# A four-layer graph network on one core: node sums in float32r, the edge softmax moved out of the main path, and another form of the attention block

## Chip, cores and metric

The kernel runs on one core of a Trainium2 chip. The metric is the time of one execution in microseconds (us) of device time. One profiled execution gives the trace that all readings below come from.

## The reference

There are 32 graphs of 512 nodes with 128 features, and one adjacency matrix of 512 x 512 zeros and ones with a full diagonal. Four layers follow each other; each ends in `x = layernorm(x + layer(x))`.

```python
# layer 0 (and layer 1 alike: other weights, no b, elu for the last leaky_relu)
h = x @ W;  e_src = h @ a_src;  e_dst = h @ a_dst
logits = leaky_relu(e_src[:, :, None] + e_dst[:, None, :], 0.2)
alpha = softmax(where(adj > 0, logits, -1e9), axis=-1)
out = leaky_relu(alpha @ h + b, 0.3)
# layer 2: an edge softmax A (512 x 512) from the edge weights e, the same for all graphs
A = softmax(where(adj > 0, e[rank of the edge], -9e15), axis=1)
out = (A * eye) @ (x @ W[0]) + (A * (1 - eye)) @ (x @ W[1]) + bias
# layer 3
y = (adj @ x + x) @ weight + bias
out = y / max(norm(y), 1e-12)
```

In the given inputs all edge weights `e` are one, so that a row of A holds the same value, one over the number of neighbours, at each edge.

## The kernel before

A graph is four chunks of 128 nodes (`NCH = 4`, 128 partitions each) of 128 features. Each graph is a Python generator, `graph(b)`, which records the instructions of one stage between two `yield`s. The loop at the end of the main path advances all running graphs by one stage per round, oldest first, and starts a new graph every second round (`STEP = 2`). So in the middle of the run, some eleven graphs are in flight, and one period of the kernel is two rounds, in which each layer's work is done for one graph. The framework's scheduler then fixes the order of each engine's queue; every engine takes its own instructions in that order, and waits on semaphores where they need another engine's result.

The stages, with their lines:

- `attention(k, b, xi)`, layers 0 and 1. Four transposes of x on TensorE (L288), a copy from PSUM on ScalarE (`xt`, L290). The product with the weights, which carry three more columns for the attention terms (`ph`, L295), and one exponential of these columns (`exps`, L297). ScalarE scales the 128 columns of h per node (L303), and GpSimd copies a column of exponentials beside them (L300). Transposes of a broadcast column give the row term (`pr`, L309). VectorE makes the 512 x 512 attention block in four steps `al` of 128x512 (L312), each the maximum of the row term and a per-node term, times the mask `mt`. Sixteen products (L318) give the weighted sums and, as column 129, their denominators. VectorE divides (L321, then L325 or L328) and applies the activation (L326, or L331 on ScalarE and L333), and GpSimd adds x (L334).
- `norm_stats` and `normalise` end each layer: statistics on VectorE (L262, L263), the power of -1/2 and the bias on GpSimd (four small instructions, L266 to L269), and four scaled copies on ScalarE (L274).
- `layer2`: products with the diagonal part `dg` of the edge softmax (L358), node sums with its other part `at` in `aggregate` (L348, `py`), copies on ScalarE (L360, L350), products with both weights (L366, L367), the bias on VectorE (L369), and x on GpSimd (L370).
- `layer3`: node sums with `a3t`, the transposed adjacency plus the identity (L348), the product (L387), the bias (L389), squares with their sum on ScalarE (L394), the norm on GpSimd (L396, L397), and the scaled sum with x on VectorE (L400).

A node sum is four products of 128x128 by 128x512 in float32. The edge softmax is worked out once, in round 5, by `edge_softmax()`, for any edge weights: ranks of the edges by running sums (L212), one-hot products (L224, L237), and a softmax of each row; `a3t` is transposed in round 9.

If an exponential leaves a wide range, or a diagonal entry is missing, the flag that `outside()` computes sends the program at its end (L614) into `general_path`, which does all graphs again in another way. With the given inputs that path does not run.

Of the kernel before, what the change touches and what calls it, by code (L numbers as in the profile page):

```python
# [23 lines left out]
F32 = mybir.dt.float32  # L25
I32 = mybir.dt.int32
AF = mybir.ActivationFunctionType
# [3 lines left out]
P = 128  # L31
# [5 lines left out]
def kernel(  # L37
# [87 lines left out]
    def attention_weights(k, w, a_src, a_dst):  # L125
# [11 lines left out]
        nc.vector.tensor_scalar(we[:, F + 2 : FE], q[:, 1:2], -0.8, None, op0=ALU.mult)  # L137
# [5 lines left out]

    exps = const.tile([P, B * 2, NCH, 3], F32, name="exps")

    def transposed(dst, src, name, add_ident=False):

        for jc in range(NCH):
            p = ps1(f"{name}_{jc}")
            for ic in range(NCH):  # L150
                nc.tensor.transpose(p[:, ic * P : (ic + 1) * P], src[:, ic, jc * P : (jc + 1) * P], ident)
            if jc % 2:
                nc.vector.tensor_copy(dst[:, jc, :], p)
            else:
                nc.scalar.copy(dst[:, jc, :], p)
            if add_ident:
                d = dst[:, jc, jc * P : (jc + 1) * P]
                nc.vector.tensor_add(d, d, ident)
# [6 lines left out]
    loops = const.tile([P, NCH, P], F32, name="loops")  # L165
    for c in range(NCH):
        nc.gpsimd.tensor_mul(loops[:, c, :], em[:, c, c * P : (c + 1) * P], ident)

    def edge_softmax():
# [63 lines left out]
        dg = const.tile([P, NCH, P], F32, name="dg")  # L233
# [19 lines left out]
        at = const.tile([P, NCH, N], F32, name="at")  # L253
        transposed(at, a, "pa")
        return at, dg

    def norm_stats(r, name, small=small):

        st = small.tile([P, NCH, 6], F32, tag="st", name=f"st{name}")
        mv = small.tile([P, NCH, 2], F32, tag="mv", name=f"mv{name}")  # L260
        for c in range(NCH):
            nc.vector.bn_stats(st[:, c, :], r[:, c, :])  # L262
            nc.vector.bn_aggr(mv[:, c, :], st[:, c, :])  # L263
        rstd = small.tile([P, NCH], F32, tag="rstd", name=f"rstd{name}", bufs=8)
        nmr = small.tile([P, NCH], F32, tag="nmr", name=f"nmr{name}", bufs=8)
        nc.gpsimd.tensor_scalar(rstd, mv[:, :, 1], EPS, None, op0=ALU.add)  # L266
        nc.gpsimd.tensor_tensor(rstd, rstd, mhalf, op=ALU.pow)  # L267
        nc.gpsimd.tensor_mul(nmr, mv[:, :, 0], rstd)  # L268
        nc.gpsimd.tensor_scalar(nmr, nmr, -1.0, None, op0=ALU.mult)  # L269
        return rstd, nmr  # L270

    def normalise(xo, r, rstd, nmr):
        for c in range(NCH):
            nc.scalar.activation(xo[:, c, :], r[:, c, :], AF.Identity, bias=nmr[:, c : c + 1], scale=rstd[:, c : c + 1])  # L274

    def new_x(k, b):
        return work.tile([P, NCH, F], F32, tag=f"x{k}", name=f"x{k}_{b}", bufs=3)

    def new_o(n):
        return work.tile([P, NCH, F], F32, tag="o", name=f"o{n}", bufs=5)  # L280


    def attention(k, b, xi):
        n = f"{k}_{b}"
        we = ATT[k]
        p = ps1(f"pt{n}")
        for c in range(NCH):
            nc.tensor.transpose(p[:, c * P : (c + 1) * P], xi[:, c, :], ident)  # L288
        xt = work.tile([P, N], F32, tag="xt", name=f"xt{n}", bufs=3)
        nc.scalar.copy(xt, p)  # L290
        yield

        ph = ps2(f"ph{n}")
        for c in range(NCH):
            nc.tensor.matmul(ph[:, c, :FE], xt[:, c * P : (c + 1) * P], we, start=True, stop=True)  # L295
        ex = exps[:, 2 * b + k]
        nc.scalar.activation(ex, ph[:, :, F:FE], AF.Exp)  # L297

        h = work.tile([P, NCH, F + 1], F32, tag="h", name=f"h{n}", bufs=3)
        nc.gpsimd.tensor_copy(h[:, :, F], ex[:, :, 1])  # L300
        for c in range(NCH):
            pc = ex[:, c, 1:2]
            nc.scalar.activation(h[:, c, :F], ph[:, c, :F], AF.Identity, bias=pc if k else 0.0, scale=pc)  # L303
        yield


        pr = ps1(f"pr{n}")
        for c in range(NCH):
            nc.tensor.transpose(pr[:, c * P : (c + 1) * P], ex[:, c, 0:1].to_broadcast([P, P]), ident)  # L309
        al = work.tile([P, NCH, N], F32, tag="al", name=f"al{n}", bufs=3)  # L310
        for j in range(NCH):
            nc.vector.scalar_tensor_tensor(al[:, j, :], pr, ex[:, j, 2:3], mt[:, j, :], op0=ALU.max, op1=ALU.mult)  # L312
        yield

        po = ps2(f"po{n}")
        for c in range(NCH):
            for j in range(NCH):
                nc.tensor.matmul(po[:, c, : F + 1], al[:, j, c * P : (c + 1) * P], h[:, j, :],  # L318
                                 start=(j == 0), stop=(j == NCH - 1))
        rs = small.tile([P, NCH], F32, tag="rs", name=f"rs{n}")  # L320
        nc.vector.reciprocal(rs, po[:, :, F])  # L321
        o = new_o(n)
        if k == 0:
# [83 lines left out]
    def graph(b):  # L407
        xi = yield from attention(0, b, X0.pop(b))
        xi = yield from attention(1, b, xi)
        if b == B - 1:  # L410
            outside()
# [235 lines left out]
```

## Time and profile before

| what | value |
|---|---|
| median of 3 runs | 797.29 us (795.61 to 797.82) |
| the profiled execution | 797.82 us; its span, first to last instruction, 796.1 us |
| granted TensorE clock, mean | 0.975 |
| TensorE products, busy | 731.8 us, 92% of the span |
| VectorE | 535.5 us, 67% |
| ScalarE | 451.7 us, 57% |
| GpSimd | 416.2 us, 52% |
| mean DMA rate | 24 GB/s |

In the lines of the profile, PE is TensorE, PEld its weight loads, DVE VectorE, ACT ScalarE, POOL GpSimd and SP the engine that issues most transfers; L12 is line 12 of the kernel file. A timeline line has the start and the length in us, then engine, line, operation, names, sizes and how many instructions were merged into it; in square brackets stands how long the engine had been idle before it, and who released it. A busy share is an average over stages with different limits: what a stage is worth is read from that stage.

### The profile page before, as it was taken

Reading aid. Unit: us, or ns where it says so; the run is one execution under the profiler, and the core shown is the slowest. Engines: PE = TensorE matmul, PEld = TensorE weight load, DVE = VectorE, ACT = ScalarE, POOL = GpSimd, SP = SyncE. Lnnn points to the kernel's source line nnn. Section 1 sums busy time; section 2 is a strip of 40 time slices with the busy share of each in tenths; the row PEclk is TensorE's granted clock in tenths of the full one; section 3 lists DMA queues with packets and bytes.
Section 4 is the critical chain, followed back from the end, with each engine's and each line's share of the span. In section 5 each row is a group of like instructions: output and inputs, shape, how many; then the busy total and the mean of one; then the engine's idle time right before and its main releaser. Section 6 shows DMA issues by size and latency. Waiting matters only on the chain. (4 is left out here: it accounts for less than half of the span.)

```text
span 796.1 us, 13784 instructions
## 1 busy us (share of the span) xinstructions
PE 731.8 (92%) x4704; PEld 580.6 (73%) x4704; DVE 535.5 (67%) x1843; ACT 451.7 (57%) x1295; POOL 416.2 (52%) x767
## 2 busy tenths in 40 slices
PE   4767999999999999999999999999999999999771
PEld 3527878777777888877777788887777777877440
DVE  4886866577776666667777766666767776757532
ACT  2214455565656666666565666666565656675352
POOL 3233345456555555555565555555656555765542
PEclk9997999999999999999999999999999999999886
DMA  4000000000000000000000000000100000000001
GB/s 132 14 14 1 28 14 14 14 17 24 28 28 28 27 28 26 16 28 28 14 28 28 28 27 28 28 14 27 28 18 24 14 15 14 14 15 27 14 27 29
DMA packets 36538, 19.28 MB, mean 24 GB/s; under 512 B 2160, under 2 KB 35952, under 8 KB 36464
## 3 DMA queue, kind: packets, MB, share of 16 engines
q1 hardware_dynamic: 34320, 17.83, 7.7%
q10 hardware_dynamic: 2144, 0.53, 0.3%
q8 instruction: 39, 0.64, 0.3%
q14 instruction: 35, 0.29, 0.1%
HBM read 9.97 MB, written 8.39 MB: 23 GB/s over the span
## 5 line engine op out<-in xcount | busy, mean ns | idle before, releaser
L274 ACT ACTIVATE x<-o,nmr,rstd 128x128 f32<-128x128 f32 x512 | 214.7, 484 | 135.0 <-POOL nmr L269 135.0
L318 PEld LDWEIGHTS po<-h,al 128*128 128x128 f32 x2048 | 237.4, 191 | 22.1 <-issue 14.9
L318 PE MATMUL po<-h,al 128*128 128x129 f32 x2048 | 244.2, 276 | 1.6 <-DVE al L312 1.2
L312 DVE SCALAR_TENSOR_TENSOR al<-pr,exps,mt 128x512 f32<-128x512 f32 x256 | 175.6, 738 | 4.0 <-PE pr L309 4.0
L267 POOL TENSOR_TENSOR rstd<-rstd,mhalf 128x4 f32<-128x4 f32 x128 | 132.9, 1038 | 10.7
L334 POOL TENSOR_TENSOR o<-o,x 128x512 f32<-128x512 f32 x64 | 82.9, 1295 | 92.1 <-DVE o L326 54.7
L262 DVE BATCH_NORM_STATS2 st<-o 128x6 f32<-128x128 f32 x512 | 128.8, 271 | 3.2 <-POOL o L334 3.2
L348 PE MATMUL py<-a3t,x 128*128 128x512 f32 x256 | 120.0, 612 | 0.1
L348 PE MATMUL py<-at,x 128*128 128x512 f32 x256 | 115.2, 593 | 0.0
L263 DVE BATCH_NORM_AGGREGATE mv<-st 128x2 f32<-128x6 f32 x512 | 85.5, 170 | 0.0
L266 POOL TENSOR_SCALAR rstd<-mv 128x4 f32<-128x4 f32 x128 | 29.1, 227 | 106.7 <-DVE mv L263 101.8
L350 ACT COPY y<-py 128x512 f32<-128x512 f32 x64 | 36.6, 573 | 84.8 <-PE py L348 84.8
L303 ACT ACTIVATE h<-ph,exps 128x128 f32<-128x128 f32 x256 | 84.1, 409 | 1.1
L348 PEld LDWEIGHTS py<-a3t,x 128*128 128x128 f32 x256 | 47.4, 195 | 49.2 <-issue 46.8
L295 PE MATMUL ph<-we,xt 128*128 128x131 f32 x512 | 70.8, 281 | 9.9 <-ACT h L303 9.2
L348 PEld LDWEIGHTS py<-at,x 128*128 128x128 f32 x256 | 46.2, 190 | 45.9 <-issue 45.9
L333 DVE SCALAR_TENSOR_TENSOR o<-t,o 128x512 f32<-128x512 f32 x32 | 22.1, 692 | 81.7 <-ACT t L331 81.7
L295 PEld LDWEIGHTS ph<-we,xt 128*128 128x128 f32 x512 | 62.2, 190 | 15.2 <-ACT h L303 14.0
L300 POOL COPY h<-exps 128x4 f32<-128x4 f32 x64 | 13.6, 213 | 100.7 <-ACT exps L297 100.7
L321 DVE RECIPROCAL rs<-po 128x4 f32<-128x4 f32 x64 | 11.6, 181 | 78.8 <-PE po L318 78.8
L290 ACT COPY xt<-pt 128x512 f32<-128x512 f32 x64 | 37.5, 586 | 32.9 <-PE pt L288 32.8
L366 PE MATMUL po<-w,y 128*128 128x128 f32 x256 | 50.7, 281 | 4.0 <-ACT y L350 4.0
(104 smaller groups left out, 947.7 us busy)
## 6 DMA issues: line engine op xcount, KB each, us to landing
x<-in_x_dram SPq DMA_DIRECT2D x32, 256.0 KB, 2.8
out_dram<-x SPq DMA_DIRECT2D x32, 256.0 KB, 2.3
an<-in_adj_dram SPq DMA_DIRECT2D x1, 1024.0 KB, 5.8
we<-in_L_gnn_W_dram ACTq DMA_DIRECT2D x2, 64.0 KB, 3.8
w<-in_L_gnn_W_dram ACTq DMA_DIRECT2D x2, 64.0 KB, 4.5
bias_b<-in_L_gnn_bias_dram ACTq DMA_DIRECT2D x2, 64.0 KB, 4.0
b_b<-in_L_gnn_b_dram ACTq DMA_DIRECT2D x1, 64.0 KB, 4.9
w_s<-in_L_gnn_weight_dram ACTq DMA_DIRECT2D x1, 64.0 KB, 3.4
```

The lines of the kernel that those rows point to most:

```text
L262: nc.vector.bn_stats(st[:, c, :], r[:, c, :])
L263: nc.vector.bn_aggr(mv[:, c, :], st[:, c, :])
L267: nc.gpsimd.tensor_tensor(rstd, rstd, mhalf, op=ALU.pow)
L274: nc.scalar.activation(xo[:, c, :], r[:, c, :], AF.Identity, bias=nmr[:, c : c + 1], scale=rstd[:, c : c + 1])
L290: nc.scalar.copy(xt, p)
L295: nc.tensor.matmul(ph[:, c, :FE], xt[:, c * P : (c + 1) * P], we, start=True, stop=True)
L303: nc.scalar.activation(h[:, c, :F], ph[:, c, :F], AF.Identity, bias=pc if k else 0.0, scale=pc)
L312: nc.vector.scalar_tensor_tensor(al[:, j, :], pr, ex[:, j, 2:3], mt[:, j, :], op0=ALU.max, op1=ALU.mult)
L318: nc.tensor.matmul(po[:, c, : F + 1], al[:, j, c * P : (c + 1) * P], h[:, j, :], start=(j == 0), stop=(j == NCH - 1))
L334: nc.gpsimd.tensor_add(o, o, xi)
L348: nc.tensor.matmul(p, xi[:, j, :], mat[:, j, :], start=(j == 0), stop=(j == NCH - 1))
L366: nc.tensor.matmul(po[:, cols], y[:, cols], w21, start=True, stop=False)
```

## The change

The change touches four things.

- The node sums of layers 2 and 3. x is split into two parts, `xh`, x rounded to float32r by a VectorE copy, and `xl`, the rest, by a GpSimd subtraction, in a stage of its own. Matrices of zeros, ones and twos (`off`, `a3t`) take the place of `at` and the former `a3t`. A node sum is then eight products in float32r, four of each part, into one PSUM tile.
- Layer 2. Its rows are now divided by the number of neighbours (`rdeg`), in four VectorE steps that also add `xb`, x plus the bias, which GpSimd makes. The diagonal part becomes x itself, transposed on TensorE.
- The edge softmax moves, unchanged, into `general_path`. `doubt()` works out whether the adjacency has other values than zero and one, a diagonal entry is missing, or the edge weights differ; `outside()` takes these into the flag.
- The attention block. `h` is no longer scaled; its copies stand in four fixed tiles `hx` whose last column is one. ScalarE makes a Relu of the row term with a per-node scale and bias from PSUM, and VectorE adds a per-node term and multiplies by the mask, both per chunk. GpSimd makes the negative bias, `nq`. In layer 0, the bias b is added to h on VectorE.

The core of the diff:

```diff
-        nc.vector.tensor_scalar(we[:, F + 2 : FE], q[:, 1:2], -0.8, None, op0=ALU.mult)
+        nc.vector.tensor_scalar(we[:, F + 2 : FE], q[:, 1:2], 0.2, None, op0=ALU.mult)
...
+    def convolution():
+        off = const.tile([P, NCH, N], F32R, name="off")
+        a3t = const.tile([P, NCH, N], F32R, name="a3t")
+        for c in range(NCH):
+            cols = slice(c * P, (c + 1) * P)
+            nc.vector.tensor_copy(off[:, c, :], mt[:, c, :])
+            nc.vector.tensor_copy(a3t[:, c, :], mt[:, c, :])
+            nc.gpsimd.tensor_mul(off[:, c, cols], mt[:, c, cols], nident)
+            nc.gpsimd.tensor_add(a3t[:, c, cols], mt[:, c, cols], ident)
+        rdeg = const.tile([P, NCH], F32, name="rdeg")
+        nc.vector.tensor_reduce(rdeg, em, axis=AX.X, op=ALU.add)
+        nc.vector.reciprocal(rdeg, rdeg)
+        return off, a3t, rdeg
+
+    def doubt():
+        loops = scratch.tile([P, NCH, P], F32, name="loops")
+        for c in range(NCH):
+            nc.gpsimd.tensor_mul(loops[:, c, :], em[:, c, c * P : (c + 1) * P], ident)
+        nc.vector.tensor_reduce(doubts[:, 0:1], loops.rearrange("p c f -> p (c f)"), axis=AX.X, op=ALU.add)
...
+        nc.vector.tensor_tensor(other, an, em, op=ALU.not_equal)
+        nc.vector.tensor_reduce(doubts[:, 1:2], other.rearrange("p c f -> p (c f)"), axis=AX.X, op=ALU.max)
+        eb = scratch.tile([P, E], F32, name="eb")
+        nc.scalar.dma_start(eb, bass.AP(tensor=e2.tensor, offset=e2.offset, ap=[[0, P], [1, E]]))
...
     def attention(k, b, xi):
...
         nc.scalar.activation(ex, ph[:, :, F:FE], AF.Exp)
+        nq = small.tile([P, NCH], F32, tag="nq", name=f"nq{n}")
+        nc.gpsimd.tensor_scalar(nq, ex[:, :, 2], -1.0, None, op0=ALU.mult)
-        h = work.tile([P, NCH, F + 1], F32, tag="h", name=f"h{n}", bufs=3)
-        nc.gpsimd.tensor_copy(h[:, :, F], ex[:, :, 1])
-        for c in range(NCH):
-            pc = ex[:, c, 1:2]
-            nc.scalar.activation(h[:, c, :F], ph[:, c, :F], AF.Identity, bias=pc if k else 0.0, scale=pc)
+        h = hx[k, b % 2]
+        if k == 0:
+            nc.vector.tensor_tensor(h[:, :, :F], ph[:, :, :F], bc(b0_b), op=ALU.add)
+        else:
+            nc.scalar.activation(h[:, :, :F], ph[:, :, :F], AF.Identity, bias=1.0)
...
         for j in range(NCH):
-            nc.vector.scalar_tensor_tensor(al[:, j, :], pr, ex[:, j, 2:3], mt[:, j, :], op0=ALU.max, op1=ALU.mult)
+            nc.scalar.activation(al[:, j, :], pr, AF.Relu, bias=nq[:, j : j + 1], scale=ex[:, j, 1:2])
+            nc.vector.scalar_tensor_tensor(al[:, j, :], al[:, j, :], ex[:, j, 2:3], mt[:, j, :], op0=ALU.add, op1=ALU.mult)
...
+        nc.vector.tensor_tensor(o, po[:, :, :F], bcol(rs), op=ALU.mult)
         if k == 0:
-            for c in range(NCH):
-                nc.vector.scalar_tensor_tensor(o[:, c, :], po[:, c, :F], rs[:, c : c + 1], b0_b, op0=ALU.mult, op1=ALU.add)
...
+    def split(xi, n):
+        xh = work.tile([P, NCH, F], F32R, tag="xh", name=f"xh{n}", bufs=3)
+        xl = work.tile([P, NCH, F], F32R, tag="xl", name=f"xl{n}", bufs=3)
+        nc.vector.tensor_copy(xh, xi)
+        nc.gpsimd.tensor_sub(xl, xi, xh.bitcast(F32))
+        return xh, xl
+
-    def aggregate(xi, mat, name):
+    def aggregate(parts, mat, n):
...
-        for j in range(NCH):
-            nc.tensor.matmul(p, xi[:, j, :], mat[:, j, :], start=(j == 0), stop=(j == NCH - 1))
+        for part in range(2):
+            for j in range(NCH):
+                nc.tensor.matmul(p, parts[part][:, j, :], mat[:, j, :], start=(part + j == 0), stop=(part + j == NCH))
...
     def layer2(b, xi):
...
-        pd = ps1(f"pdx{n}")
-        for c in range(NCH):
-            nc.tensor.matmul(pd[:, c * P : (c + 1) * P], xi[:, c, :], dg[:, c, :], start=True, stop=True)
+        parts = split(xi, n)
+        pt = ps1(f"pt{n}")
+        for c in range(NCH):
+            nc.tensor.transpose(pt[:, c * P : (c + 1) * P], xi[:, c, :], ident)
...
+        xb = work.tile([P, NCH, F], F32, tag="xb", name=f"xb{n}", bufs=2)
+        nc.gpsimd.tensor_tensor(xb, xi, bc(bias2_b), op=ALU.add)
+        yield
+        y = aggregate(parts, off, n)
...
-        nc.vector.tensor_tensor(o, chunks(po), bc(bias2_b), op=ALU.add)
-        nc.gpsimd.tensor_add(o, o, xi)
+        for c in range(NCH):
+            nc.vector.scalar_tensor_tensor(o[:, c, :], po[:, c * P : (c + 1) * P], rdeg[:, c : c + 1], xb[:, c, :],
+                                           op0=ALU.mult, op1=ALU.add)
...
     def layer3(b, xi):
...
-        y = aggregate(xi, a3t, n)
+        parts = split(xi, n)
+        yield
+        y = aggregate(parts, a3t, n)
...
         elif r == 5:
-            at, dg = edge_softmax()
-            CONV = (load_w(w2[0], "w20"), load_w(w2[1], "w21"), load_row(bias2, "bias2_b"), at, dg)
-        elif r == 9:
-            a3t = const.tile([P, NCH, N], F32, name="a3t")
-            transposed(a3t, an, "pa3", add_ident=True)
-            AGG = (load_w(w3, "w3_s"), load_row(bias3, "bias3_b"), a3t)
+            off, a3t, rdeg = convolution()
+            CONV = (load_w(w2[0], "w20"), load_w(w2[1], "w21"), load_row(bias2, "bias2_b"), off, rdeg)
+            AGG = (load_w(w3, "w3_s"), load_row(bias3, "bias3_b"), a3t)
+        elif r == 30:
+            doubt()
```

## The prediction

> **What bounds the kernel now.** I read the busy shares of the steady stretch first. The columns are stretch, its length, then busy time of TensorE, its weight loads, VectorE (DVE), ScalarE (ACT) and GpSimd (POOL), granted clock, DMA share, GB/s:
>
> ```profile
> 400.00:500.00 100.00, 98.67 (x644) 78.69 (x645) 72.36 (x254) 61.04 (x179) 56.18 (x103) 1.00 0.09 25
> 740.00:760.00 20.00, 15.42 (x55) 9.57 (x54) 7.75 (x39) 10.18 (x30) 11.07 (x23) 0.83 0.05 14
> ```
>
> TensorE has no spare time in the middle; at the end it waits, at a lower clock. Its timeline gives the period: the same products of two graphs that follow each other start 22.0 us apart, and the node sums (L348) take 3.5 and 3.4 us of that.
>
> ```profile
> 400.05 1.16 PE L295 MATMUL ph<-we,xt 128*128 128x131 f32 x8 [0.32 <-ACT h L303]
> 405.24 3.67 PE L348 MATMUL py<-a3t,x 128*128 128x512 f32 x8
> 408.75 1.05 PE L358 MATMUL pdx<-dg,x 128*128 128x128 f32 x8
> 409.64 3.60 PE L348 MATMUL py<-at,x 128*128 128x512 f32 x8
> 422.04 1.16 PE L295 MATMUL ph<-we,xt 128*128 128x131 f32 x8 [0.33 <-ACT h L303]
> ```
>
> The list of waits shows that the other engines already hand work to each other in series, and are only covered by TensorE:
>
> ```profile
> ACT x L274 <- POOL nmr L269: 135.0, 95, 7.8
> POOL rstd L266 <- DVE mv L263: 101.8, 66, 4.7
> ```
>
> Two timelines near the end show a collision. Three L400 instructions took 0.85 us in the steady stretch (at 412.96) and 1.87 us here, where a GpSimd addition of 512 columns ran beside them:
>
> ```profile
> 751.89 1.87 DVE L400 SCALAR_TENSOR_TENSOR o<-o,ss,x 128x128 f32<-128x128 f32 x3
> ...
> 752.05 1.30 POOL L370 TENSOR_TENSOR o<-o,x 128x512 f32<-128x512 f32 x1 [1.26 <-DVE o L369]
> ```
>
> **What the Trainium skill says.** (1) "FP8 and Floating Point Precision", TensorE Precision Notes: true fp32 takes four passes through the array, a reduced form cuts the number on reading. The trace agrees on fp32: a 512-column product is two records of 0.429 us, together 0.857; no run here shows the reduced form. (2) "SBUF — State Buffer", Who interferes with whom: a VectorE instruction with two SBUF inputs, or in a two-port mode, and a GpSimd instruction that reads SBUF exclude each other for a whole instruction. The pair above agrees: 1.0 us lost. (3) "ScalarE: Activation LUTs", What ACT_TABLE_LOAD costs: each per-partition scale or bias adds about 93 ns. The trace agrees: four L303 took 1.14 us with one such operand and 1.48 with two, 85 ns each. (4) "VectorE: DVE Perf Modes", the tier table: an fp32 copy inside SBUF runs at double rate, from PSUM not; L242, a scalar operation of 128x512 in SBUF, took 0.417 us, the PSUM copy L153 0.692.
>
> **The change, by engine, per graph** (pitch in us, from instructions that follow each other; shares are means of the five stretches of 100 us from 200 to 700). *TensorE*: 98.6% of 22.0 is 21.7. The diagonal product (0.89) becomes four transposes (0.44). The node sums, 6.94, become 16 products of one pass; a quarter of 0.857 is 0.214, so 3.43. Result 17.7. No row shows float32r, so it is bounded by one pass (17.7) and two (21.1); I take one. *ScalarE*: 62.9% of 22.0 is 13.8; eight scaled copies (84.1/32 = 2.6) go, one 512-column copy comes (0.66), and eight Relu from PSUM with two operands: 0.43 (one L303 with two) plus 384 columns at 0.83 ns is 0.75, pitch 0.67, 5.4 in all. Result 17.3. *VectorE*: 70% is 15.4. The eight al steps keep their number and 0.66 pitch, but read al and mt, two SBUF inputs, where L312 read PSUM and SBUF. The copy h of layer 0 adds 0.61; L325 saves 0.44; the layer-2 bias costs 0.44 more as four; two xh copies add 0.33 each. Result 16.7. *GpSimd*: 57.3% is 12.6. nq replaces the copy L300, xb replaces the addition L370, the two xl subtractions add 2 x 1.27. Result 15.2. DMA queues: two small loads of e become one, w3 and bias3 are loaded earlier, the loads of x and stores of out on SP are unmoved; at a DMA share of 0.09 I put this at nothing.
>
> So no engine alone needs more than 17.7. What decides is the order in the queues. In the built program's order, VectorE has the next graph's al steps behind the statistics of layer 0 (st_17 ahead of al_15); in the kernel before, L312 stands ahead of L262 and the loop below isn't closed. Those statistics wait for GpSimd's addition o_17, which stands behind nq_18, which waits for exps_18 on ScalarE, behind the normalisation x_11 of layer 2, which waits for GpSimd's rstd_11, behind xb_13 and xl_13 of the next layer-2 input and rstd_8 of layer 3, which wait for VectorE. One turn of this loop, in us:
>
> - VectorE: al x4 2.64, rest of statistics 0.36, xh 0.33, al x4 2.64, layer-2 o x4 1.05, mv 0.08, layer-3 o x4 1.05, its statistics 1.20, reciprocal and mv 0.37: 9.7.
> - GpSimd: rstd group 2.03 (414.27 to 416.30), xb 1.35, nq 0.28, xl 1.35, rstd group 1.95: 7.0.
> - ScalarE: x 1.62, exps 0.17: 1.8. GpSimd: nq 0.28, addition 1.27: 1.55. VectorE: statistics 1.70. Four hand-overs of 0.04 to 0.07: 0.25.
>
> The sum is 22.0, as long as TensorE's period now. To it comes the lock: xl of layer 3 is released by xh, just as four al steps begin, and takes the port after the first of them: 0.95 (the 1.0 above, less its start). xl of layer 2 waits for the ELU step, which xb has held back: 0.55. Small GpSimd operations behind two-input steps: 0.2 (L268 took 0.42 there and 0.20 elsewhere). Period 23.7. The price of the lock has ends of 0 and 3. Less than nothing is ruled out: a port that is shared can't speed either side. What TensorE saves is hidden: it would idle 6 us a turn, waiting for al.
>
> **Outside the steady stretch.** Taking every eighth L312, which is one graph, the kernel before is 166.0 us of start, 23 periods of 22.0, and 124.3 of end: 796.1, its span. *Start*: graph work on TensorE stops from 34.3 to 68.2 for the edge softmax: 33.9, and the 16 transposes of a3t (2.1) go too. Against this, latencies of the first graphs that hid in the stop come back (after it, stages followed at 5.4 to 5.8, before it at up to 7.6: about 6), and VectorE gets a comparison and a reduction of 2048 columns (2.3 each, as L173), eight copies (2.7) and small reductions (1), of which some 4 delays al. So 166 less 26, 140; bounds 133 and 146. *End*: layers 2 and 3 each get a stage (xh 0.33, xl 1.27, hand-over), 3.4 together; the last node sums save as much at full clock. I take 126, bounds 118 and 132.
>
> Sum: 140 + 23 x 23.7 + 126 = 811. The profiled execution took 797.8, 1.7 more than its span, and lies 0.5 above the median, 797.3. So **812 us**.
>
> **Rivals.** *The lock costs little* (the other side): the program's al steps keep VectorE's port, or xl falls into gaps. Then the period is the bare 22.0 and the time 140 + 506 + 126 + 2 = 774, faster by the softmax alone. It decides below a period of 23.0, that is, when the lock costs under 1.0 us a turn. For it: in the steady stretch now, GpSimd's L334 and L370 mostly fall beside L312, L325 and L369, and lose nothing. Against: the release of xl by xh puts it beside al in every turn. 0.26. *TensorE remains the bound*: if the loop is slack at some hand-over, the period is near 18 and the time 682. Against: the order in the queues closes the loop. 0.06. *float32r takes two passes*, so the change does not do what it says: TensorE's 21.1 then lies partly inside the loop (the reciprocal waits for po, 1.7 later), period about 24.5, time 832. 0.10. *The idle array loses clock*: the last stretch shows 0.83 at three quarters busy; at 0.83, 17.7 is 21.3, with the same result as the former, 832. 0.08. The forecast itself: 0.50.
>
> **Numbers.** A measurement of this kernel tells some 0.3% from no change. Of the forecast, 0.06 lies within 0.3% of no change and the rest above: slower 0.62, same 0.06, faster 0.32. The range reaches from period 22 with the short start and end (133 + 506 + 126 + 2 = 767) to period 25.2 (140 + 580 + 126 + 2 = 848). The case of a slower kernel has its own range of 800 to 848.
>
> **What would show it.** Right: the distance between graphs is 23 to 25 us; TensorE is busy about 75% and waits for al; al steps of over 1.2 us beside GpSimd subtractions; ScalarE's x still waits for nmr; no 34 us stop at the start; float32r products follow each other at 0.21 us. Wrong: a period under 23.0, al steps all near 0.7, products at 0.43, or TensorE above 95% busy.

## Result and profile after

The changed kernel takes **844.99 us** (842.27 to 845.68), the kernel before 796.86 us in the same comparison: ratio **1.060, 95% interval 1.057 to 1.063**. The forecast said slower, 812 us; the slowdown is 48 us and not 15. The profiled execution took 844.4 us with a span of 842.6. Split as in the forecast, by every eighth al step (L268 now):

| | forecast | measured |
|---|---|---|
| start, to the eighth graph's al | 140 | 154.6 |
| 23 periods | 545 (23.7 each) | 547.5 (23.9 each in the steady part) |
| end, from the 31st graph's al | 126 | 140.5 |
| span | 811 | 842.6 |

The steady stretch came out close to what was worked out. Of the 31.6 us by which the span is above 811, the start has 14.6, the end 14.5 and the 23 periods 2.5.

Busy time in the middle and near the end (columns as before: stretch, length, PE, PEld, DVE, ACT, POOL, clock, DMA share, GB/s):

```profile
400.00:500.00 100.00, 88.38 (x602) 79.93 (x601) 77.45 (x242) 70.27 (x173) 75.39 (x106) 0.86 0.08 23
790.00:810.00 20.00, 14.77 (x76) 12.63 (x75) 10.44 (x52) 10.62 (x35) 10.59 (x20) 0.84 0.09 27
```

No engine is full any more, and TensorE runs at 0.86 of its clock in the middle, where it was at 1.00. Its timeline, the products that were shown of before:

```profile
398.79 1.06 PE L248 MATMUL ph<-we,xt 128*128 128x131 f32 x8
...
404.98 1.18 PE L311 MATMUL py<-off,xh 128*128 128x512 f32 x4
405.99 1.08 PE L311 MATMUL py<-off,xl 128*128 128x512 f32 x4
406.91 0.60 PE L264 MATMUL pr<-ident,exps 128*128 128x128 f32 x4
407.35 0.60 PE L241 MATMUL pt<-ident,x 128*128 128x128 f32 x4
410.26 1.07 PE L264 MATMUL pr<-ident,exps 128*128 128x128 f32 x4 [2.32 <-DVE o L359]
...
413.97 2.06 PE L311 MATMUL py<-a3t,xh 128*128 128x512 f32 x4
415.82 1.68 PE L311 MATMUL py<-a3t,xl 128*128 128x512 f32 x4
...
422.69 1.06 PE L248 MATMUL ph<-we,xt 128*128 128x131 f32 x8
```

Two graphs follow each other at 23.9 us. The float32r sum with `off` takes 1.93 us (404.98 to 406.91): one record per product, 0.23 to 0.25 us each, so a single pass, as forecast (0.214). The sum with `a3t`, same shapes, takes 3.37: 0.42 us each, about half speed. That is the lower clock, seen in one place: the granted clock is 0.50 from 410.28 to 417.11 and 1.00 before and after. Just before, TensorE stood for 2.3 us (407.95 to 410.26).

The list of waits (engine, line, releaser: us in total, times, longest):

```profile
ACT x L227 <- POOL nmr L222: 173.7, 73, 7.3
POOL rstd L219 <- DVE mv L216: 112.4, 87, 4.6
...
PE pr L264 <- DVE o L359: 50.1, 22, 2.3
...
DVE rs L277 <- PE po L274: 32.6, 42, 5.0
```

The hand-overs that TensorE covered before are now the path. The shared port shows where the forecast put it, in VectorE's and GpSimd's timelines:

```profile
415.37 3.76 DVE L268 SCALAR_TENSOR_TENSOR al<-al,exps,mt 128x512 f32<-128x512 f32 x4
...
415.60 1.66 POOL L303 TENSOR_TENSOR xl<-x,xh 128x512 fp32r<-128x512 f32 x1 [0.72 <-DVE xh L302]
```

Four al steps take 3.76 us beside `xl`; the four before them, at 412.07 in the next fence, take 2.72 with nothing but small GpSimd instructions beside them: 1.0 us lost. In the steady part one al step a turn takes about 1.78 us, the others about 0.75. GpSimd's small instructions lose too; in its timeline, with VectorE's ELU step (425.67) between:

```profile
423.54 1.04 POOL L220 TENSOR_TENSOR rstd<-rstd,mhalf 128x4 f32<-128x4 f32 x1
...
425.67 1.44 DVE L287 SCALAR_TENSOR_TENSOR o<-t,o 128x512 f32<-128x512 f32 x1 [0.64 <-ACT t L285]
...
426.53 0.66 POOL L252 TENSOR_SCALAR nq<-exps 128x4 f32<-128x4 f32 x1
427.16 1.26 POOL L303 TENSOR_TENSOR xl<-x,xh 128x512 fp32r<-128x512 f32 x1
...
428.81 1.53 POOL L220 TENSOR_TENSOR rstd<-rstd,mhalf 128x4 f32<-128x4 f32 x1
```

The power (L220) takes 1.04 us, and 1.53 beside VectorE's L281, which starts at 428.75; `nq` takes 0.66 here and 0.22 at 408.88 below.

**One turn of the loop.** Followed back over one turn, from each instruction to the later of the one before it in its queue and those it waits for, the chain is this (timelines of four engines, in order of time):

```profile
408.64 0.16 ACT L250 ACTIVATE exps<-ph 128x12 f32<-128x12 f32 x1
408.88 0.22 POOL L252 TENSOR_SCALAR nq<-exps 128x4 f32<-128x4 f32 x1 [0.60 <-ACT exps L250]
409.07 1.27 POOL L288 TENSOR_TENSOR o<-o,x 128x512 f32<-128x512 f32 x1
...
412.07 2.72 DVE L268 SCALAR_TENSOR_TENSOR al<-al,exps,mt 128x512 f32<-128x512 f32 x4
412.86 1.46 PE L274 MATMUL po<-hx,al 128*128 128x129 f32 x4 [0.60 <-DVE al L268]
...
419.56 3.29 PE L274 MATMUL po<-hx,al 128*128 128x129 f32 x28
422.89 0.18 DVE L277 RECIPROCAL rs<-po 128x4 f32<-128x4 f32 x1 [0.16 <-PE po L274]
423.23 0.23 POOL L219 TENSOR_SCALAR rstd<-mv 128x4 f32<-128x4 f32 x1 [0.44 <-DVE mv L216]
...
430.98 1.26 ACT L227 ACTIVATE x<-o,nmr,rstd 128x128 f32<-128x128 f32 x3 [3.80 <-POOL nmr L222]
```

ScalarE 0.24, GpSimd 1.49, VectorE's statistics 1.70 and one al step 0.79, **TensorE 10.03** (412.86 to 422.89), VectorE 0.34, GpSimd 7.75, ScalarE's x 1.56: 23.9. The forecast went from al to the reciprocal through VectorE's own queue. That branch is there too, 10.82 us from 412.07, of which VectorE stands only 0.36 waiting for TensorE. TensorE's branch, with the half-speed node sum between two parts of `po`, ends 0.36 later. It wasn't in the forecast.

### The profile page after: what moved, and what is told of

Read it like the earlier page. It is cut to its first block, busy times and chain, and to the rows that moved or that the text cites. A ratio compares the mean times of both kernels' runs of the same rounds, so it can differ in the third digit from the quotient of the medians.

```text
span 842.6 us, 13666 instructions
## 1 busy us (share of the span) xinstructions
PE 687.2 (82%) x4504; PEld 616.6 (73%) x4504; DVE 607.6 (72%) x1894; ACT 541.6 (64%) x1315; POOL 564.4 (67%) x823
## 5 line engine op out<-in xcount | busy, mean ns | idle before, releaser
L227 ACT ACTIVATE x<-o,nmr,rstd 128x128 f32<-128x128 f32 x512 | 211.9, 485 | 173.9 <-POOL nmr L222 173.7
L274 PE MATMUL po<-hx,al 128*128 128x129 f32 x2048 | 277.8, 291 | 42.9 <-DVE al L268 40.0
L274 PEld LDWEIGHTS po<-hx,al 128*128 128x128 f32 x2048 | 256.8, 202 | 61.6 <-DVE al L268 40.7
L268 DVE SCALAR_TENSOR_TENSOR al<-al,exps,mt 128x512 f32<-128x512 f32 x256 | 202.3, 849 | 2.9 <-ACT al L267 2.9
L267 ACT ACTIVATE al<-pr,nq,exps 128x512 f32<-128x512 f32 x256 | 179.5, 796 | 3.4 <-PE pr L264 1.5
L220 POOL TENSOR_TENSOR rstd<-rstd,mhalf 128x4 f32<-128x4 f32 x128 | 163.5, 1277 | 10.3
L303 POOL TENSOR_TENSOR xl<-x,xh 128x512 fp32r<-128x512 f32 x64 | 91.7, 1433 | 20.2 <-DVE xh L302 17.6
L264 PE MATMUL pr<-ident,exps 128*128 128x128 f32 x256 | 49.2, 325 | 56.6 <-DVE o L359 50.1
L311 PE MATMUL py<-a3t,xh 128*128 128x512 f32 x128 | 62.0, 632 | 8.7 <-ACT t L364 4.5
L364 ACT ACTIVATE t<-o 128x128 f32<-128x128 f32 x128 | 39.9, 340 | 43.8 <-DVE o L359 33.5
L370 DVE SCALAR_TENSOR_TENSOR o<-o,ss,x 128x128 f32<-128x128 f32 x128 | 36.1, 342 | 34.3 <-POOL ss L367 34.3
L333 PEld LDWEIGHTS po<-w,y 128*128 128x128 f32 x256 | 47.4, 221 | 14.0 <-ACT y L313 10.5
```

Source lines behind the costliest of these rows:

```text
L267: nc.scalar.activation(al[:, j, :], pr, AF.Relu, bias=nq[:, j : j + 1], scale=ex[:, j, 1:2])
L268: nc.vector.scalar_tensor_tensor(al[:, j, :], al[:, j, :], ex[:, j, 2:3], mt[:, j, :], op0=ALU.add, op1=ALU.mult)
L303: nc.gpsimd.tensor_sub(xl, xi, xh.bitcast(F32))
L333: nc.tensor.matmul(po[:, cols], y[:, cols], w21, start=True, stop=False)
```

## Experiments

All ratios are to the kernel before, with 95% intervals; start, mean of 23 periods and end as above; clock in the stretch 400 to 500. The column us is the median; the terms and the clock are those of one profiled execution, which lies within 4 us of it (f32_sums' 3.7 below, noyield's 3.9 above). Wherever an edit is made without holding the queues, the scheduler makes an order of its own, so that most pairs of rows differ in the order too.

| kernel | us | ratio | start | period | end | clock |
|---|---|---|---|---|---|---|
| before | 797 | 1 | 166.0 | 22.0 | 124.3 | 1.00 |
| changed | 845.0 | 1.060 (1.057 to 1.063) | 154.6 | 23.8 | 140.5 | 0.86 |
| soft_only | 767.2 | 0.963 (0.960 to 0.966) | 133.0 | 22.4 | 116.8 | 1.00 |
| f32_sums | 790.3 | 0.991 (0.989 to 0.993) | 148.4 | 22.6 | 117.4 | 1.00 |
| old_att | 871.7 | 1.094 (1.091 to 1.096) | 127.8 | 26.1 | 141.9 | 0.83 |
| relu_out | 838.8 | 1.053 (1.050 to 1.055) | 132.8 | 24.7 | 138.1 | 0.88 |
| noyield | 819.6 | 1.027 (1.024 to 1.030) | 150.9 | 23.9 | 122.1 | 0.86 |
| old_noy | 796.8 | 1.000 (0.998 to 1.001) | 133.4 | 23.7 | 119.2 | 0.86 |
| psum_al | 867.4 | 1.088 (1.086 to 1.091) | 147.3 | 25.3 | 134.3 | 0.90 |
| after_pq | 934.2 | 1.170 (1.167 to 1.174) | 153.3 | 28.0 | 136.8 | 0.88 |
| xl_dve | 826.5 | 1.037 (1.034 to 1.040) | 153.9 | 23.5 | 132.4 | 0.95 |
| warm | 830.4 | 1.041 (1.037 to 1.044) | 154.6 | 23.3 | 140.3 | 1.00 |
| rev | 794.8 | 0.997 (0.996 to 0.998) | 140.5 | 22.8 | 128.9 | 1.00 |
| old_rev | 719.2 | 0.902 (0.901 to 0.904) | 118.7 | 20.5 | 127.1 | 0.98 |
| norm_dve | 812.0 | 1.018 (1.015 to 1.021) | 138.4 | 23.5 | 132.0 | 0.98 |
| best_try | 743.8 | 0.932 (0.930 to 0.935) | 131.1 | 21.5 | 117.9 | 0.95 |
| add_noy | 738.6 | 0.927 (0.924 to 0.930) | 133.5 | 21.3 | 116.0 | 0.98 |
| best_rev | 687.2 | 0.862 (0.858 to 0.865) | 121.2 | 19.4 | 117.4 | 1.00 |

### The parts of the change: soft_only, old_att, f32_sums

Attention block old or new, node sums in float32 or in two float32r parts; the softmax is moved in all. The edits are the hunks of the diff, undone:

```diff
 # soft_only, old_att: the attention block of before
 ...
-            nc.scalar.activation(al[:, j, :], pr, AF.Relu, bias=nq[:, j : j + 1], scale=ex[:, j, 1:2])
-            nc.vector.scalar_tensor_tensor(al[:, j, :], al[:, j, :], ex[:, j, 2:3], mt[:, j, :], op0=ALU.add, op1=ALU.mult)
+            nc.vector.scalar_tensor_tensor(al[:, j, :], pr, ex[:, j, 2:3], mt[:, j, :], op0=ALU.max, op1=ALU.mult)
 ...
 # soft_only, f32_sums: off and a3t in float32, no split, no yield after it
-        parts = split(xi, n)
-        yield
-        y = aggregate(parts, a3t, n)
+        y = aggregate(xi, a3t, n)
```

> The changed kernel with the attention block of the kernel before (max form from PSUM, h scaled on ScalarE) and plain float32 node sums without the split in two parts; what is left of the change is the edge softmax moved out and layer 2 with 1/degree. Theory (closed loop of queues plus shared port): nothing of the loop's lengthening is here, TensorE needs 21.3 us a graph and bounds again, period 21.3 to 22.0; the start term falls by the 26 us of the forecast, 140 to 144, end 122 to 127; 755 to 775 us. Rival (the start loss comes from taking out the stop itself, as the first graphs then run through cold queues): start term 150 or more with any attention form, 780 us. Rival (the moved softmax alone accounts for the slowdown): 840 us.

> The changed kernel with the attention block of the kernel before; the float32r sums, the split and the moved softmax stay. Theory (closed loop plus shared port): the al steps read PSUM, so VectorE no longer has two SBUF inputs there and xl can't shut it out; ScalarE loses the 5.4 us of Relu. Period 19 to 21.5, start 140 to 146, end 124 to 134; 705 to 760 us, faster than the kernel before. Rival (the split and its extra stages set the period and the two terms): period stays at 23 to 24, 820 us or more. Rival (the idle array loses clock and so keeps the time): TensorE clock at or under 0.86 and period about 22.

> The changed kernel with plain float32 node sums: no split (no xh, no xl, and the two extra stages gone with it); the new attention block and the moved softmax stay. Theory: GpSimd's two subtractions of 1.35 leave the loop, and so does the lock beside al; the rest of the loop is about 19.5 and TensorE needs 21.3, so TensorE bounds again: period 21.5 to 22.5, start 142 to 152, end 126 to 134; 770 to 800 us. Rival (the new attention block itself sets the period, the port has no part): period 23.5 to 24, 830 us or more.

The totals of soft_only and f32_sums lie in their ranges, with TensorE 95% and 97% busy at full clock. Not every term does: soft_only's start is 7 us and its end 5 below what was expected, its period 0.4 above; f32_sums' end is 9 below. Busy time of f32_sums:

```profile
400.00:500.00 100.00, 97.22 (x630) 76.23 (x629) 69.89 (x248) 74.62 (x185) 63.03 (x107) 1.00 0.07 22
```

old_att missed by over 110 us. It has no Relu, no two-SBUF al step, and a period of 26.1. Its busy time:

```profile
400.00:500.00 100.00, 76.50 (x519) 69.69 (x517) 63.66 (x223) 51.05 (x153) 56.90 (x94) 0.83 0.07 22
```

No engine above 77%. So a theory that needs the new al step for the long loop falls. The clock is at 0.83, as the rival of the idle array had it, but the period is not that rival's 22. What the slow kernels share so far is the split sums; old_rev below has them too and is fast. The four kernels also split the other two terms. **Start**: taking the stop out gives 166.0 to 133.0 (soft_only); the new attention block costs 15.4 us (133.0 to 148.4) or, with the split, 26.8 (127.8 to 154.6). **End**: the split costs 25.1 (116.8 to 141.9) and 23.1 (117.4 to 140.5), the attention block 0.6 and -1.4.

### The start: relu_out

```diff
-            nc.scalar.activation(al[:, j, :], pr, AF.Relu, bias=nq[:, j : j + 1], scale=ex[:, j, 1:2])
-            nc.vector.scalar_tensor_tensor(al[:, j, :], al[:, j, :], ex[:, j, 2:3], mt[:, j, :], op0=ALU.add, op1=ALU.mult)
+            nc.vector.scalar_tensor_tensor(al[:, j, :], pr, ex[:, j, 2:3], mt[:, j, :], op0=ALU.max, op1=ALU.mult)
```

> The changed kernel without the Relu on ScalarE and without nq on GpSimd: the al step is the single instruction of the kernel before (max of pr and a column, times the mask, from PSUM). The column and h stay those of the changed kernel, so the attention weights are other ones: the Relu form is left out of the computation. Theory for the start: the Relu stands in ScalarE's queue ahead of the next graph's xt, and it alone makes the fill slow: start 126 to 136, as old_att (127.8). Rival (the rest of the new block does, that is h with its two memory sets and copies, and the early work for the node sums): start stays at 148 or more. No claim on the period, which depends on the new order: 23 to 27 by the other kernels with the split.

The start falls to 132.8, 21.8 less, as expected. The place was not the one named. TensorE's timeline of the changed kernel, then ScalarE's:

```profile
21.01 1.13 PE L248 MATMUL ph<-we,xt 128*128 128x131 f32 x4
21.94 4.34 PE L274 MATMUL po<-hx,al 128*128 128x129 f32 x26
26.12 0.61 PE L248 MATMUL ph<-we,xt 128*128 128x131 f32 x4
...
26.77 0.18 ACT L250 ACTIVATE exps<-ph 128x12 f32<-128x12 f32 x1 [5.81 <-PE ph L248]
```

ScalarE's `xt` starts at 20.37 here and at 20.25 in relu_out, so the Relu doesn't hold it back. Half of the second graph's `ph` stands behind thirteen products of the first graph's `po`, and its exponentials come at 26.77; in relu_out, whose queue has all of `ph` ahead of most of `po`, at 22.30. Whether the Relu's time or the order that was made around it costs the fill is not separated by this run. rev below keeps the Relu and has a start of 140.5.

### The end: noyield and old_noy

```diff
         parts = split(xi, n)
-        yield
         y = aggregate(parts, a3t, n)
 # and the same in layer 2; old_noy: with the attention block of before
```

> The changed kernel without the two yields that follow the split in layer 2 and layer 3: the node sums are issued in the same stage as the split, so a graph has two stages, that is one turn, fewer between its first al and its end. Theory for the end term: a stage costs half a turn of the loop, not its own latency, so the end term falls by one period, from 140.5 to 114 to 120; start 150 to 156; period 22.5 to 24.5, because the scheduler makes a new order; 790 to 835 us. Rival (the stages cost their own latency of 1.7 each, as the prediction had it): end term 136 to 138, 840 us.

> old_att without the two extra stages after the split: attention block of the kernel before, float32r sums, moved softmax. Theory: end term one turn shorter than old_att, 116 to 124; start 126 to 132; period depends on the order that the scheduler makes, 21.5 to 24; 735 to 800 us. Rival (old_att's period of 26.1 comes from the split and not from its order): period stays at 26, 850 us.

The end falls by 18.4 us in the one (140.5 to 122.1) and by 22.7 in the other (141.9 to 119.2), while the two stages' own work stays. The rival, 1.7 us a stage, is out. A graph advances two stages a turn. With two stages more, its end lies one turn further behind its al, and a turn is 23.9 and 26.1 us. Measured are 5.5 and 3.4 us less than a turn; that the turns get shorter at the end may be why, which is not shown. The end of noyield is 2 above the range. old_noy's period of 23.7 also shows that old_att's 26.1 does not come from the split alone.

### The port, at one order of the queues: psum_al and after_pq

```diff
 # psum_al
-... al[:, j, :], ex[:, j, 2:3], mt[:, j, :], op0=ALU.add, op1=ALU.mult)
+... al[:, j, :], ex[:, j, 2:3], pr, op0=ALU.add, op1=ALU.mult)
 # after_pq: the changed kernel; edges without semaphores between neighbours put
 # the queues of all engines in psum_al's order
+        for a, b in zip(order, order[1:]):
+            tc.add_manual_dep(q[b], q[a].name, info, reason="queue order")
```

> The changed kernel with one operand changed: the second operand of the al step is pr in PSUM in place of the mask mt in SBUF, so that the step has one SBUF input; the mask is left out of the computation. Number and sizes of all instructions stay. Theory: the lock goes, the four al steps beside xl take about 2.7 us in place of 3.76, period 22.0 to 22.6; start and end terms each some 3 to 8 lower; 790 to 810 us. Rival (the loop without any lock is 23.9 long): no change, 840 us or more. Rival (the lock is also what stretches fill and drain): start under 145 and end under 130, 780 us.

> The changed kernel, every instruction as it is, but with the queues of all five engines in the order in which they stand in psum_al (order given by edges without semaphores). Compared with the changed kernel only the order differs; compared with psum_al only the second operand of the al steps (mask in SBUF here, PSUM there). Theory now: the order of the queues sets the loop, and the shared port adds to it: period that of psum_al, 25.3, plus 0.5 to 2, so 25.8 to 27.3; pow on GpSimd back from 1.03 to over 1.2 us; 875 to 910 us. Rival (psum_al is slow because al reads pr and holds its PSUM buffer longer, not for its order): period back to 23.9, 845 us. Rival (the port costs nothing): period 25.3, 867 us.

psum_al missed: slower, 867 us. One operand had been changed, but the scheduler made another order from it. That is why after_pq was run. Groups of both from 300 to 600 us (count, busy us, mean ns), psum_al first:

```profile
L268 DVE SCALAR_TENSOR_TENSOR al<-al,exps,pr 128x512 f32<-128x512 f32 x95 | 68.8, 744 | 5.1 <-ACT al L267 4.9
...
L220 POOL TENSOR_TENSOR rstd<-rstd,mhalf 128x4 f32<-128x4 f32 x48 | 49.6, 1034 | 4.0
```

```profile
L440 DVE SCALAR_TENSOR_TENSOR al<-al,exps,mt 128x512 f32<-128x512 f32 x86 | 67.5, 815 | 4.4 <-ACT al L439 4.4
...
L392 POOL TENSOR_TENSOR rstd<-rstd,mhalf 128x4 f32<-128x4 f32 x43 | 48.3, 1124 | 3.6
```

At one order, the second SBUF operand makes al 815 ns instead of 744, the power 1124 instead of 1034, and the period 28.0 instead of 25.3: 2.6 us a turn. It is not the operand by itself: the al steps with no GpSimd instruction beside them take 745 ns and 740 on average. All GpSimd instructions together take 1.8 us a turn more, the eight al steps 0.6. But TensorE's `po` products take 1.5 more as well, at a clock of 0.88 instead of 0.90, so the 2.6 us are the port and what follows from it, the clock included. Period and total, 934, are above the ranges given, and the power is below the 1.2 expected. And the same instructions as in the changed kernel, in this order, take 28.0 a turn instead of 23.8: **order alone is worth 4.2 us a turn** here.

### xl on VectorE: xl_dve

```diff
-        nc.gpsimd.tensor_sub(xl, xi, xh.bitcast(F32))
+        nc.vector.tensor_sub(xl, xi, xh.bitcast(F32))
```

> The changed kernel with the two subtractions of the split on VectorE instead of GpSimd. VectorE gets 2 x 0.66 more, GpSimd loses 2 x 1.3 and with them the port conflict of xl with al and with the ELU step. Theory (closed loop plus port): GpSimd's part of the loop shortens by one or two subtractions and the lock by 1.1 to 1.5 us, so period 21.8 to 23.0 in spite of VectorE's added work, start 145 to 152, end 128 to 138; 785 to 820 us. Rival (port conflict not decisive, VectorE work is): period 24 to 25, 850 us or more.

A miss: the period falls by only 0.3, to 23.5. al takes 746 ns on average instead of 874, so its part of the conflict is gone. But a new order came with it, so the run says little on the port.

### The clock: warm

```diff
+        if k == 0:
+            for d in range(6):
+                nc.tensor.matmul(ph[:, d % NCH, 160:256], ident, mt[:, 0, :96], start=True, stop=True)
 # and the queues held in the changed kernel's order, these six ahead of pr
```

> The changed kernel in its own order of queues, with six float32 products of 96 columns added on TensorE in each layer-0 attention, into columns of the ph buffer that nothing reads, at the place where TensorE otherwise sits idle for 2.3 us a turn (ahead of pr). Nothing waits for them. In the changed kernel's trace TensorE runs at half clock after that stop: the node sum of layer 3 takes 3.37 us for eight products instead of 1.9, between the al step and the attention product, and VectorE's reciprocal waits for that product; VectorE's own path is only 0.36 us shorter. Theory (both paths close the loop, VectorE's with the port conflict is the next): the clock rises, the eight products take 1.9 to 2.6, the period falls by no more than 0.4 to 0.5, to 23.4 to 23.6; 832 to 842 us. Rival (the idle array's clock alone sets the period): 21.9 to 22.6, 800 to 815 us. Rival (six products don't hold the clock): no change in period, 843 to 850 us.

More work on TensorE makes the kernel faster: 830.4 us, ratio 1.041 against 1.060; the total is 1.6 us below the range. Start and end stay as they were. Busy time, and the rows that answer to the loop above, VectorE's and TensorE's:

```profile
400.00:500.00 100.00, 84.88 (x642) 77.83 (x641) 75.69 (x245) 69.74 (x174) 75.53 (x106) 1.00 0.08 24
```

```profile
453.66 2.72 DVE L450 SCALAR_TENSOR_TENSOR al<-al,exps,mt 128x512 f32<-128x512 f32 x4
455.42 1.19 PE L493 MATMUL py<-a3t,xh 128*128 128x512 f32 x4
456.45 1.10 PE L493 MATMUL py<-a3t,xl 128*128 128x512 f32 x4
456.96 3.75 DVE L450 SCALAR_TENSOR_TENSOR al<-al,exps,mt 128x512 f32<-128x512 f32 x4
...
463.96 0.16 DVE L459 RECIPROCAL rs<-po 128x4 f32<-128x4 f32 x1
```

The clock is 1.00, the node sum is back at 2.1 us, and the reciprocal no longer waits. The loop is now the forecast's own, without TensorE: VectorE 10.61 from al to the last mean and variance, GpSimd 7.73, ScalarE 1.80, GpSimd 1.49, statistics 1.69: 23.3. So in the changed kernel the idle array's clock costs 0.6 us a turn, a little above the 0.4 to 0.5 expected; the other 23.3 are the loop through VectorE's branch, port conflict included (al takes 870 ns on average in warm, 874 in the changed kernel).

One more sign stands in the clock record. TensorE's clock changes only on a grid of 3.41 us (last section). In the changed kernel two such steps at half clock begin every 23.89 us, which is seven steps, and the graphs follow each other at the same 23.89. So they do in the steady part of noyield and old_noy, though these have other orders and their al steps are not stretched (738 and 732 ns on average). One period in three different kernels looks as if the clock's grid holds it; a run without the half-clock steps, warm, was made of the changed kernel alone.

### Order alone: rev and old_rev

```diff
-        running = [g for g in running if next(g, running) is None]
+        running = [g for g in running[::-1] if next(g, running) is None][::-1]
```

> The changed kernel with one line different: in each round the stages of the running graphs are issued youngest graph first, where they were issued oldest first. No instruction is added, removed or moved to another engine; only the order in the queues differs. Theory (order of the queues sets the loop, and the fill's pace): other loop, period 22.5 to 24, start 138 to 148 since young graphs are served first, end 125 to 135; 785 to 830 us. Rival (the order doesn't matter, the work does): 840 to 850 us.

> old_att with the same one line: youngest graph first. Against old_att (871.7 us, period 26.1) only the order differs. Theory: the loop of old_att comes from its order; period 21 to 22.5, start 115 to 125, end 122 to 132; 730 to 770 us. Rival (the split itself costs it): 26, 860 us or more.

The same instructions on the same engines, youngest graph first in each round: the changed kernel goes from 845 to **794.8 us**, old_att from 872 to **719.2**, below the range given. Start, period and end all fall in both. The rivals, that the work or the split itself sets the time, are out: these kernels have the same. The order is no third cause beside the port and the clock: in rev the al steps take 738 ns on average and the power 1.04 us (874 ns and 1.34 in the changed kernel), and the clock is 1.00. Part of what the order does is to decide whether these prices are paid.

### Versions built to beat both: norm_dve, best_try, add_noy, best_rev

```diff
 # norm_dve; best_try = old_noy with it
-            nc.scalar.activation(xo[:, c, :], r[:, c, :], AF.Identity, bias=nmr[:, c : c + 1], scale=rstd[:, c : c + 1])
+            nc.vector.tensor_scalar(xo[:, c, :], r[:, c, :], nmr[:, c, 0:1], rstd[:, c : c + 1], op0=ALU.subtract, op1=ALU.mult)
 # add_noy = old_noy with
-        nc.gpsimd.tensor_add(o, o, xi)
+        nc.vector.tensor_add(o, o, xi)
 # best_rev = add_noy, youngest graph first, and
-        nc.vector.tensor_copy(xh, xi)
+        nc.scalar.copy(xh, xi)
```

> The changed kernel with the normalisation on VectorE (subtract the mean, multiply by rstd: four steps of 128 columns in SBUF) in place of ScalarE, which leaves GpSimd two small instructions (eps, pow) instead of four, and no nmr. Takes some 0.6 us of each GpSimd group and 1.1 us of each normalisation out of the loop, adds 1.7 to 2 us a graph to VectorE. Theory (closed loop of queues): period 20.5 to 22, start 138 to 146, end 118 to 128; 730 to 780 us, though VectorE does more. Rival (VectorE or ScalarE throughput sets the period): VectorE has more to do, period 24 to 26, 850 us or more. Rival (TensorE at a lower clock sets it): 23.9 stays.

> All that the theory asks for together: moved edge softmax and float32r sums of the changed kernel, attention block of the kernel before, no extra stages after the split, normalisation on VectorE. Theory: TensorE needs 17.7 us a graph, the loop about 20, start 125 to 132, end 106 to 112; 690 to 720 us, faster than the kernel before and than soft_only. Rival (the split can't be hidden in any order): 765 us or more.

> old_noy with the two residual additions of the attention layers on VectorE in place of GpSimd (2 x 0.66 more on VectorE, 2 x 1.3 less on GpSimd, and the statistics no longer wait for GpSimd). Theory: the link VectorE statistics after GpSimd addition, which closed the loop, is gone; period 20 to 21.5, start 126 to 132, end 112 to 120; 705 to 745 us. Rival (VectorE becomes the bound as in norm_dve): VectorE over 97% busy, period 22 or more, 760 us.

> add_noy with youngest graph first and the copy xh on ScalarE (0.35 us less on VectorE per node sum, and no hand-over between the normalisation and xh). Theory: a shorter loop, TensorE's 17.7 us come within reach: period 19.3 to 20.8, start 115 to 126, end 114 to 124; 680 to 725 us, the fastest of all. Rival (VectorE, 90% busy in add_noy, bounds in any order): period 21 or more, 735 us.

norm_dve missed and beats only the changed kernel: VectorE is full instead. Part of that is the port: its al steps take 983 ns on average, where rev's take 738, some 2 us a turn. Its busy time, and best_rev's:

```profile
400.00:500.00 100.00, 84.01 (x613) 74.12 (x613) 100.00 (x323) 44.33 (x103) 64.47 (x73) 0.98 0.08 25
```

```profile
400.00:500.00 100.00, 94.62 (x724) 86.25 (x723) 90.56 (x317) 74.30 (x216) 71.45 (x119) 1.00 0.10 28
```

best_try has the same trouble (VectorE 97%, 744 us where 690 to 720 was expected). add_noy keeps the normalisation on ScalarE and lies in its range. best_rev, 687 us and 14% below the kernel before, differs from add_noy in the order and in the engine of `xh`, which are not told apart; it has TensorE as its fullest engine again, 95% busy at full clock, and a period of 19.4, below the 21.3 us a graph that float32 sums would need on TensorE (an estimate: the forecast's 21.7, less 0.89 and plus 0.44).

## Why the forecast was right and wrong

- **What failed: the start and end terms.** They were put too low by 14.6 and 14.5 us, which is 29.1 of the 31.6 us of the span; the two bullets on them below name the steps.
- **Direction, and the loop of the steady part: right but for one branch.** The loop of queues that was named is there: its VectorE branch was put at 9.7 + 0.95 = 10.65 and is 10.61 in warm, and GpSimd's 7.0 + 0.55 + 0.2 = 7.75 is 7.73. The steady stretch is 547.5 us after 545.
- **The price of the lock: right in size, not in all places.** `xl` beside al costs 1.0 (forecast 0.95). On GpSimd, the forecast had `xl` of layer 2 lose 0.55 to the ELU step and small operations 0.2. That `xl` is no longer than it was put (1.34, put at 1.35); `nq`, put at 0.28, takes 0.63 behind the ELU step, and the second rstd group 2.48 instead of 1.95, its power 1.53 instead of 1.04. That the sums agree is luck in part. What the Trainium skill says ("SBUF — State Buffer", Who interferes with whom) agrees with these and with the longer al and GpSimd steps of after_pq beside psum_al.
- **Missed in the loop: TensorE's branch.** The step "What TensorE saves is hidden: it would idle" let the idle array keep its speed. It runs at half speed after a stop of 2.3 us a turn, and 0.6 of the 23.9 us comes from that. The rival that the idle array loses clock was right in the fact and too high in the size. The forecast's own loop runs at 23.3 (warm), 0.4 below its 23.7; the branch that was missing made up for that, so the period agrees partly by luck. The 23.89 may also be held by the clock's grid, which is not shown.
- **The signs named were there:** x waits for `nmr`, 173.7 us in all; the stop of 34 us is gone; float32r products at 0.23 to 0.25 us; one al step a turn takes about 1.78 us beside `xl`. TensorE is busy 88% and not about 75%, since part of its work runs at half speed; in warm, at full clock, it would be some 78% without the added products (an estimate: 84.88 less 1.58 us in each 23.3).
- **The start term failed: 140, measured 154.6.** The step is "166 less 26", which counts the stop against latencies and VectorE's extra work, and lets the fill go on otherwise at the pace of before. Removing the stop was worth more, 33.0 net in soft_only. The new attention block in the fill was left out, that is, put at nothing, and costs 15.4 without the split and 26.8 with it. From soft_only's 133.0, the block adds 15.4 and the split then 6.2 to make 154.6. Whether the block costs by its own time or by the order made around it stays open: rev has the same block and 140.5.
- **The end term failed: 126, measured 140.5.** The step is "layers 2 and 3 each get a stage, 3.4 together". The split costs 23.1 at the end (f32_sums to changed), of which taking out the two stages gives back 18.4: a stage was priced at its own latency and costs the better part of half a turn. The other 4.7 are near the 3.4. The rest of the change lowers the end by 6.9 (124.3 to 117.4), where the forecast put the last node sums' saving against the 3.4.
- **The order was taken as given.** The forecast read the order in the built program, and for that order it was right to say "slower"; but it said so of a change whose instructions, in another order, take 794.8 us (rev), within 0.3% of the kernel before. Against the rivals: TensorE as the bound, 682 us, did not come about; best_rev, which is near it, needs the attention block of before, another order, no stage after the split, two additions moved off GpSimd and `xh` on ScalarE. Two passes are out (0.23 us a product). The lock costing little is out.

Left open: how much of the start is the Relu's own time. A kernel with the changed one's order of queues and without the second SBUF operand was not tried, since that order needs `pr`'s buffer back before the al steps that would read it.

## What to carry to other kernels

Where no engine is full, a stage is priced in turns of the loop, not in its own latency: a new yield moved the end by 9 to 11 us here, somewhat less than half a turn, for 1.7 us of work. Split a forecast into start, period and end, and price each changed part in all three; in the fill here a new step had little to hide behind. Before an instruction is blamed, hold the order of the queues and change it alone, or change the order alone: here one line of order was worth 50 us in one kernel and 152 in another.

## What the runs showed of the hardware

- TensorE's granted clock has two values in the eighteen traces, 1.00 and 0.50, and changes only on a grid of 3.41 us. Taken step by step, by the time in which a product was under way in the trace: all 307 full-clock steps with under 1.4 us of work were followed by half clock, and none of the 2642 with 2.5 us or more; all 333 half-clock steps with 3.2 us or more were followed by full clock, and one of the 272 with under 2.8.
- In the changed kernel, the step from 406.87 to 410.28 has 1.1 us of work and the stop of 2.3 us in it; half clock follows for 6.8 us, and eight 512-column float32r products take 3.37 us instead of 1.93. The Trainium skill ("TensorE: Matmul & The Clock Gate", Part 1) has the two states, but names an idle window of about 3.4 us for the fall; here a window that was idle for two thirds was enough, and six small products in the stop kept the clock at 1.00.
- A power of 128x4 values on GpSimd took 1.53 us beside VectorE's L281, a step with two SBUF inputs, and 1.04 in the same turn without such a step beside it.
